# The end of the 3x3 stage: last banks divided by output half, one half's row sums added by TensorE

## The chip, the cores and the metric

One core of one Trainium2 chip runs the whole program. The metric is the device time of one execution in microseconds (us); lower is better. All arithmetic is fp32.

## The reference

Two ResNet bottleneck layers in sequence, on x of 64 x 1024 x 14 x 14, each with its own weights and with batch statistics (mean and variance over all 64 images and all pixels):

```
def _bn(x, gamma, beta):
    mean = jnp.mean(x, axis=(0, 2, 3), keepdims=True)
    var = jnp.var(x, axis=(0, 2, 3), keepdims=True)
    xn = (x - mean) * jax.lax.rsqrt(var + EPS)
    return gamma.reshape(1, -1, 1, 1) * xn + beta.reshape(1, -1, 1, 1)
out = jax.nn.relu(_bn(_conv(x, w1, b1, 1, 0), g1, be1))      # 1x1, 1024 -> 256
out = jax.nn.relu(_bn(_conv(out, w2, b2, 1, 1), g2, be2))    # 3x3,  256 -> 256
out = _bn(_conv(out, w3, b3, 1, 0), g3, be3)                 # 1x1,  256 -> 1024
out = jax.nn.softplus(residual_scale)[0] * out
return jax.nn.relu(x + out)
```

Because a norm needs the statistics of its whole input, no 1x1 product behind the 3x3 convolution can begin before the last pixel of the 3x3 convolution is summed and its statistics are merged. The change lies at exactly that border, which the program crosses twice, once in each layer.

## The kernel before

The 256 channels lie as 128 partitions x 2 halves (`MS` = 2; `o` is the output half, `s` the input half). The tile `y_all` holds all 256 channels of all pixels in SBUF, first the input of the 3x3 convolution and then, written back in place, its output. Images go in 8 groups of 8 (`NG` = 8, `GI` = 8).

`conv2` is the 3x3 stage. Along the rows it works with six combinations (`NF` = 6) of input rows, each multiplied with its own transformed filters; four output rows (`RT` = 4 tiles of rows, `out_rows[0]` to `out_rows[3]` and the bottom row `end`) are then sums and differences of the six products. The combinations come in pairs, in the order (1, 2), (3, 4), (5, 0), so combination 0 of group 7 is the last of the stage. Along the columns a product is done with even and odd output columns (`EVEN`, `ODD`, the index `q`): one product of sums (`m`), one of differences (`l`), and two more that are accumulated in PSUM onto a copy of `m`.

For one combination (`Products`) the pieces are these. `open` takes the PSUM tile `columns`: two banks of 512 fp32 values per partition, two such tiles in rotation. `start` makes `m` and `put` lets ScalarE copy it into both banks. `middle` makes `l`, and `bring` copies it with both signs to the SBUF tile `ls`. `columns` (the method) accumulates eight matmuls of 224 columns, two for each pair (`q`, `o`), into the banks; for the last combination it goes by output half (`across`): both `q` of `o` = 0, then both of `o` = 1. The trace counts two TensorE records for each fp32 matmul. Before the change the first index of the tile, the bank, is `q`, and the two output halves lie side by side in each bank.

`finish` is a generator that is sent each finished combination and forms the output rows. In the last group it pins the order of its VectorE work (`run`) and of ScalarE's (`act`), by hand. There `a` (tile `fa`) holds the sum of combinations 1 to 4, and `d` (tile `fb`) their weighted differences. Combination 5 completes `d` (line 1083), whose batch statistics are taken (`stat`, lines 1026 and 1085), and `merge` turns the sums of squares of the other rows into entries of the same table with GpSimd. Then combination 0, `cb`, completes `a`: line 1088 adds `cb.ls`, and lines 1089 to 1093 add the banks:

```
for o in range(MS):
    for q in EVEN, ODD:
        v = halves(a[:, o : o + 1])[:, q]
        run(nc.vector.tensor_add(v, v, cb.banks[:, q, o].rearrange("p (l c) -> p l c", c=WH)))
    stat(1, o, a)
```

Lines 1094 to 1097 let ScalarE copy the rows `d3`, `d[:, :, full]` and `a` to `y_all`. Meanwhile TensorE, which has nothing to compute, runs six matmuls of the identity into the tiles `m` (line 1240, `busy`).

Behind the stage `aggregate` (line 2079) merges the table with one `bn_aggr` for each output half, and `affine` makes scale and shift of it: a square root on ScalarE (`sd`, line 2095), then a row of small VectorE instructions (lines 2096 to 2127). The first rows of `y` are normed with them, on ScalarE (line 343, called through `norm`) and on VectorE (line 1595 in layer 0, 1353 in layer 1), and then the products of the third convolution start on TensorE (tiles `cy`, `cx`, `cp`).

Instructions that are neither pinned by `run` nor by `act` or `matmul` are put in an order by the framework, by their dependencies and by when they can be ready; it also inserts all waits between engines, from what each instruction reads and writes. `matmul` and `act` are helpers, so most TensorE work has line 168 and most ScalarE work line 343; go by the tile names.

Of the kernel before, what the change touches and what calls it, by code (L numbers as in the profile page):

```python
# [11 lines left out]
AF = mybir.ActivationFunctionType  # L12
# [7 lines left out]
MS = M // P  # L20
# [54 lines left out]
def bottlenecks(ctx: ExitStack, tc: tile.TileContext, x, w1s, w2s, w3s, pars, out):  # L75
# [633 lines left out]
    def conv2(b, par, aff, early, rest):  # L709
# [8 lines left out]
        def columns():  # L718

            return psum.pool.tile([P, 2, 512], FP, tag="columns", name="columns", bufs=2)  # L720
# [39 lines left out]
        class Inputs:  # L760
# [3 lines left out]
            def __init__(self, pair, run=lambda ins: None, copy=nc.scalar.activation):  # L764
                self.pair, self.run, self.copy = pair, run, copy
                self.tiles = tiles = full if pair[0] == 3 else RT
                self.lines = lines = tiles * GI
                n = len(pair) * MS * lines

                def part(tag, width):  # L770
                    v = place(tag, 2 * MS * RT * GI * width)
                    return v[:, : n * width].rearrange("p (k s l c) -> p k s l c", k=2, s=MS, c=width)

                self.r, self.v = part("r", W), part("v", W)
                self.sums, self.diffs = part("sums", WH), part("diffs", WH)
# [30 lines left out]
            def products(self, g, k):  # L806
                i = self.pair[k]

                first = g == 0 and i == order[0][0]
                u = {}  # L810
                for tag, a, e in ("ua", 0, 1), ("ub", 1, NK):
                    alone = made[tag] % BUFS[tag] == 0
                    made[tag] += 1
                    v = pool.tile(
                        [P, MS * MS * (e - a) * P], FP, tag=tag + "_first" * alone, name=tag, bufs=1 if alone else BUFS[tag] - 1
                    )
                    v = v.rearrange("p (s o k m) -> p s o k m", s=MS, o=MS, m=P)
                    for part in [slice(1, 2), slice(0, 1)] if g == 0 and i in order[0] else [slice(0, MS)]:
                        nc.sync.dma_start(
                            out=v[:, part].rearrange("p s o k m -> p (s o) (k m)"),  # L820
                            in_=us[b][i][:, part, :, a:e].rearrange("p s o k m -> p (s o) (k m)"),
                        )
                    u[a] = v
                return Products(i, self.lines, self.v[:, k], self.sums[:, k], self.diffs[:, k], u, first)

        def two_rows(g, s):
            v = y_all[:, s, g * GPX : g * GPX + 4 * full * LINE]
# [80 lines left out]
        class Products:  # L908


            def __init__(self, i, lines, r, sums, diffs, u, first):
                self.i, self.lines, self.n = i, lines, lines * WH
                self.r, self.sums, self.diffs, self.u, self.first = r, sums, diffs, u, first

            def bank(self, tag):
# [27 lines left out]

            def open(self):
                self.ls = None
                self.banks = columns()[:, :, : MS * self.n].rearrange("p q (o n) -> p q o n", o=MS)

            def fill(self):

# [66 lines left out]
        def finish():  # L1016


            for g in range(NG):
                out_rows = [y_grp[:, :, g, k::4, :] for k in range(4)]  # L1020
                last_group = g == NG - 1

                by_transfer = g < NG - 2

                def stat(k, o, v):
                    run(nc.vector.bn_stats(stats[:, o, 1 + k, :], v[:, o].rearrange("p r l -> p (r l)")))

                def run(ins):
                    tc.keep_in_program_order(ins)

                ca = yield
                fa = outputs(ca)
                if g == 1:
                    begin(y_grp[:, :, 0, 1 : 4 * full : 4, :])
                fb = outputs((yield))
                a, d = new("fa"), new("fb")
                nc.vector.tensor_add(a, fa, fb)
                nc.vector.tensor_sub(d, fa, fb)

                fa = outputs((yield))  # L1040
                fb = outputs((yield))
                c, e = new("fc", full), fa
                nc.vector.tensor_add(c, fa, fb)
                nc.vector.tensor_sub(e, fa, fb)
                a3, d3 = (v[:, :, :full] for v in (a, d))
                end = y_grp[:, :, g, H - 1]

                def middle_rows():

                    for o in range(MS):  # L1050
                        stt(out_rows[1][:, o, :full], e[:, o], 2.0, d3[:, o])
                        stt(out_rows[2][:, o], c[:, o], 4.0, a3[:, o])

                def outer_rows():

                    if by_transfer:

                        nc.vector.tensor_add(out_rows[0][:, :, :full], a3, c)
                        act(out_rows[0][:, :, full], a[:, :, full], AF.Copy)
                    else:  # L1060
                        nc.vector.tensor_add(a3, a3, c)
                    if by_transfer:

                        for o in range(MS):
                            stt(out_rows[3][:, o], e[:, o], 8.0, d3[:, o])
                        act(end, d[:, :, full], AF.Copy)
                    else:
                        stt(d3, e, 8.0, d3)

                if g > 1:  # L1070
                    middle_rows()
                    outer_rows()
                if last_group:
                    for o in range(MS):
                        lines = y_grp[:, o, g, 1 : 1 + 4 * full].rearrange("p (r k) l -> p r k l", k=4)[:, :, :2]
                        for k in range(2):
                            moment(lines, idle[:, : 2 * full * LINE].rearrange("p (r k l) -> p r k l", k=2, l=LINE), o, k, g)

                ca = yield
                if last_group:  # L1080

                    for v in ca.ls, ca.banks:
                        run(nc.vector.tensor_add(halves(d), halves(d), ca.by_columns(v)))
                    for o in range(MS):
                        stat(0, o, d)
                    merge()
                    cb = yield
                    run(nc.vector.tensor_add(halves(a), halves(a), cb.by_columns(cb.ls)))
                    for o in range(MS):
                        for q in EVEN, ODD:  # L1090
                            v = halves(a[:, o : o + 1])[:, q]
                            run(nc.vector.tensor_add(v, v, cb.banks[:, q, o].rearrange("p (l c) -> p l c", c=WH)))
                        stat(1, o, a)
                    act(out_rows[3], d3, AF.Copy)
                    act(end, d[:, :, full], AF.Copy)
                    for o in range(MS):
                        act(out_rows[0][:, o], a[:, o], AF.Copy)
                    continue
                fa = outputs(ca)
                if g < 2:  # L1100
                    outer_rows()

                if by_transfer:
                    for o in range(MS):
                        nc.gpsimd.dma_start(out=out_rows[3][:, o], in_=fa[:, o, :full], accum_op=ALU.add)  # L1105
                    nc.gpsimd.dma_start(out=end, in_=fa[:, :, full], accum_op=ALU.add)
                else:
                    nc.vector.tensor_add(out_rows[3], d3, fa[:, :, :full])
                    nc.gpsimd.tensor_add(end, d[:, :, full], fa[:, :, full])

                cb = yield
                if g < 2:
                    middle_rows()
                if by_transfer:

                    f = outputs(cb)
                    for o in range(MS):
                        nc.gpsimd.dma_start(out=out_rows[0][:, o], in_=f[:, o], accum_op=ALU.add)
                    continue
                nc.vector.tensor_add(halves(a), halves(a), cb.by_columns(cb.ls))  # L1120
                for q in (EVEN, ODD):
                    for o in range(MS):
                        to, more = (
                            v[:, o].rearrange("p r (i q c) -> p q r i c", i=GI, q=2)[:, q] for v in (out_rows[0], a)
                        )
                        nc.vector.tensor_add(to, cb.banks[:, q, o].rearrange("p (r i c) -> p r i c", r=RT, c=WH), more)
            yield
# [95 lines left out]
        for k in range(1, NG * NF):  # L1223
# [13 lines left out]
            item.columns(*qs, across=not more)  # L1237
            finished.send(item)
            queue = queue[1:] + list(itertools.islice(coming, k > 1))
        busy(psum, "m", 6)  # L1240

    def conv3(psum, t, o, w3, tag=None):
        ps = psum.tile(tag=tag)
# [1149 lines left out]
```

## Time and profile before

| what | us |
|---|---|
| median of 3 runs | 1884.51 |
| lowest and highest of them | 1884.0, 1885.09 |
| the profiled execution's own time | 1884.64 |
| its span, first to last instruction | 1882.9 |
| TensorE busy | 1867.9 (99% of the span) |
| VectorE busy | 1572.3 (84%) |
| ScalarE busy | 1111.8 (59%) |
| GpSimd busy | 744.1 (40%) |

Outside the span lie 1.7 us of the profiled execution. The stage ends at about 578.6 us of the span in layer 0 and at 1505.2 us in layer 1. A duration in a profile row belongs to one instruction or, with "xN", to N of them in a row; what stands in brackets behind it is idle time of that engine just before, and what ended it. In the chain of waits each piece is what the next one waited for.

### The profile page before, as it was taken

How to read it: one execution, taken by the hardware profiler on the slowest of the kernel's cores; microseconds unless marked ns; L12 is line 12 of the kernel's file. 1: busy time of each engine (PE TensorE's matmuls, PEld its weight loads, DVE VectorE, ACT ScalarE, POOL GpSimd, SP SyncE). 2: the span in 40 equal slices, each digit the busy share in tenths (PEclk: the TensorE clock that was granted, in tenths of full speed). 3: DMA queues.
4: the chain of work that ended last, by engine and by line, in shares of the span. 5: the costliest groups of instructions: out<-in, count | busy, mean ns of one | idle time of the engine just before them, and what ended most of it. 6: DMA issues, size and time to landing. Idle time of an engine off the chain costs nothing.

```text
span 1882.9 us, 28622 instructions
## 1 busy us (share of the span) xinstructions
PE 1867.9 (99%) x9728; PEld 1555.8 (83%) x9728; DVE 1572.3 (84%) x2494; ACT 1111.8 (59%) x2329; POOL 744.1 (40%) x763
## 2 busy tenths in 40 slices
PE   9999999999999999999999999999999999999999
PEld 5555557999998998899999999999999977555555
DVE  5787867999998776778878888899999987888887
ACT  2222214677777665555555555457777795766666
POOL 0111100121205655377677776301121051776665
PEclk9999999999999999999999999999999999999999
DMA  7777654797765556678788787559788466999997
GB/s 290 270 253 271 215 187 130 209 216 218 208 195 170 185 170 215 244 277 315 269 280 314 272 319 272 209 166 220 215 208 223 138 177 215 337 378 338 356 337 269
DMA packets 246754, 458.88 MB, mean 244 GB/s; under 512 B 41472, under 2 KB 213008, under 8 KB 233552
## 3 DMA queue, kind: packets, MB, share of 16 engines
q1 hardware_dynamic: 208432, 375.30, 59.1%
q0 software_dynamic: 31328, 29.18, 8.0%
q10 hardware_dynamic: 6848, 52.57, 6.9%
q8 instruction: 77, 1.26, 0.3%
q14 instruction: 69, 0.57, 0.1%
HBM read 289.44 MB, written 141.03 MB: 229 GB/s over the span
## 4 chain that ended last, share of the span: by engine, by line
PE 93%; DVE 4%; ACT 1%; issue 1%; POOL 0%; DMA 0%; ACTq 0%; SPq 0%; DVEq 0%; POOLq 0%
PE ay L168 20%; PE cy L168 16%; PE columns L168 13%; PE ap L168 13%; PE cp L168 8%; PE m L168 6%; PE l L168 6%; PE cx L168 5%; PE ax L168 4%; PE ps L168 1%; ACT y L343 0%; DMA x<-in_x 0%; DVE f L1004 0%; DVE v L796 0%; DVE y L751 0%
## 5 line engine op out<-in xcount | busy, mean ns | idle before, releaser
L168 PE MATMUL columns<-v,ub 128*128 128x224 f32 (+1 forms) x1536 | 303.4, 339 | 1.3 <-ACT columns L343 0.8
L343 ACT ACTIVATE x<-x,shift 128x392 f32<-128x392 f32 x444 | 255.2, 613 | 66.2 <-DVE x L537 31.4
L168 PEld LDWEIGHTS columns<-v,ub 128*128 128x128 f32 x1536 | 268.5, 188 | 8.3 <-ACT columns L343 1.5
L343 ACT ACTIVATE cu<-cy,scale 128x196 f32<-128x196 f32 (+1 forms) x360 | 175.6, 500 | 163.3 <-PE cy L168 156.2
L168 PE MATMUL ay<-at,ws 128*128 128x196 f32 (+1 forms) x760 | 191.6, 383 | 0.4 <-ACT au L343 0.2
L668 POOL TENSOR_TENSOR x<-x,cu 128x392 f32<-128x392 f32 x120 | 126.8, 1058 | 103.8 <-DVE x L537 68.2
L168 PEld LDWEIGHTS ay<-at,ws 128*128 128x128 f32 x760 | 134.8, 190 | 35.7 <-issue 1.0
L537 DVE SCALAR_TENSOR_TENSOR x<-cp,scale,x 128x196 f32<-128x196 f32 (+1 forms) x240 | 124.4, 518 | 42.0 <-PE cp L168 40.7
L343 ACT ACTIVATE au<-ay 128x196 f32<-128x196 f32 (+1 forms) x139 | 53.6, 386 | 169.6 <-PE ay L168 159.8
L168 PE MATMUL l<-diffs,ub 128*128 128x224 f32 (+1 forms) x768 | 149.7, 337 | 0.4 <-DVE diffs L804 0.3
L168 PE MATMUL m<-sums,ua 128*128 128x224 f32 (+1 forms) x752 | 146.0, 336 | 1.2 <-issue 0.6
L168 PEld LDWEIGHTS l<-diffs,ub 128*128 128x128 f32 x768 | 134.5, 189 | 1.8 <-DVE diffs L804 1.1
L1105 POOL DMA_DIRECT2D y<-f x24 | 32.1, 1635 | 258.4 <-DVE f L1004 258.4
L168 PEld LDWEIGHTS m<-sums,ua 128*128 128x128 f32 x752 | 131.4, 189 | 2.6 <-issue 0.9
L168 PE MATMUL cx<-y,w 128*128 128x196 f32 (+1 forms) x404 | 124.7, 395 | 0.0
L560 POOL TENSOR_TENSOR x<-x,cu 128x196 f32<-128x196 f32 (+1 forms) x120 | 104.9, 874 | 47.1 <-ACT cu L343 19.5
L168 PE MATMUL cy<-y,w 128*128 128x196 f32 (+1 forms) x372 | 115.5, 397 | 1.7 <-ACT y L343 0.9
L343 ACT ACTIVATE y<-y,shift,scale 128x320 f32<-128x320 f32 (+9 forms) x105 | 110.2, 1074 | 7.1 <-DVE shift L2127 6.4
L565 POOL TENSOR_TENSOR x<-x,cu 128x392 f32<-128x392 f32 x60 | 80.4, 1340 | 84.6 <-DVE x L537 81.9
L215 POOL DMA_DIRECT2D u<-y x48 | 26.0, 545 | 210.9 <-ACT y L343 210.1
L964 ACT ACTIVATE columns<-m 128x448 f32<-128x448 f32 (+1 forms) x144 | 70.8, 492 | 56.1 <-PE m L168 49.0
L1976 POOL TENSOR_SCALAR y<-y,scale 128x392 f32<-128x392 f32 x57 | 92.4, 1622 | 28.4 <-DVE scale L2334 28.4
(334 smaller groups left out, 4516.4 us busy)
## 6 DMA issues: line engine op xcount, KB each, us to landing
ub<-u SPq DMA_DIRECT2D x92, 768.0 KB, 5.4
x<-in_x SPq DMA_DIRECT2D x35, 1568.0 KB, 8.0
x<-mid SPq DMA_DIRECT2D x31, 1568.0 KB, 8.7
mid<-x ACTq DMA_DIRECT2D x30, 1568.0 KB, 9.3
out<-x SPq DMA_DIRECT2D x120, 392.0 KB, 7.1
x<-in_x SPq DMA_DIRECT2D x108, 392.0 KB, 7.9
ua<-u SPq DMA_DIRECT2D x92, 256.0 KB, 3.1
z<-kept SPq DMA_DIRECT2D x60, 392.0 KB, 3.0
```

The costliest lines, as they stand in the source:

```text
L168: tc.keep_in_program_order(nc.tensor.matmul(*args, **kw))
L215: nc.gpsimd.dma_start(out=us[b][i][:, s, o], in_=u)
L343: tc.keep_in_program_order(nc.scalar.activation(*args, **kw))
L537: run(nc.vector.scalar_tensor_tensor(v, bank, self.scale[:, o : o + 1], v, ALU.mult, ALU.add))
L560: run(nc.gpsimd.tensor_add(self.part(1, 1), self.part(1, 1), u3))
L565: run(nc.gpsimd.tensor_add(v, v, self.u12))
L668: nc.gpsimd.tensor_add(v, v, self.u12[:, i * self.n : (i + 1) * self.n])
L964: copy(v, m, AF.Copy)
L1105: nc.gpsimd.dma_start(out=out_rows[3][:, o], in_=fa[:, o, :full], accum_op=ALU.add)
L1976: run(nc.gpsimd.tensor_scalar(z, z, scale[:, o : o + 1], None, ALU.mult))
```

## The change

The last combination's two banks are divided by output half instead of by column parity: bank 0 holds both parities of `o` = 0, bank 1 those of `o` = 1. For `o` = 0, two matmuls of the identity with `a` (one for each parity) accumulate the row sums into bank 0, so that the finished row stands in PSUM; its `bn_stats` reads the bank, and ScalarE copies it from the bank to `y_all` in two pieces. For `o` = 1, VectorE adds bank 1 to `a` in one instruction instead of two, and takes the statistics and the copy from SBUF as before. Half 1 now comes ahead of half 0. `busy` runs four matmuls of the identity instead of six. The same code runs in both layers.

```
--- before.py
+++ after.py
@@ products
+                last = (g, i) == (NG - 1, order[-1][-1])
+                return Products(i, self.lines, self.v[:, k], self.sums[:, k], self.diffs[:, k], u, first, last)
...
@@ open
-                self.banks = columns()[:, :, : MS * self.n].rearrange("p q (o n) -> p q o n", o=MS)
+                v = columns()[:, :, : MS * self.n]
+                if self.last:
+                    self.banks = v.rearrange("p o (q n) -> p q o n", q=2)
+                else:
+                    self.banks = v.rearrange("p q (o n) -> p q o n", o=MS)
...
@@ finish, last group
                     run(nc.vector.tensor_add(halves(a), halves(a), cb.by_columns(cb.ls)))
-                    for o in range(MS):
-                        for q in EVEN, ODD:
-                            v = halves(a[:, o : o + 1])[:, q]
-                            run(nc.vector.tensor_add(v, v, cb.banks[:, q, o].rearrange("p (l c) -> p l c", c=WH)))
-                        stat(1, o, a)
+                    in_bank = [cb.banks[:, :, o].rearrange("p q (l c) -> p q l c", c=WH) for o in range(MS)]
+                    for q in EVEN, ODD:
+                        matmul(
+                            in_bank[0][:, q], ident, halves(a[:, :1])[:, q], start=False, stop=True, skip_group_check=True
+                        )
+                    v = halves(a[:, 1:])
+                    run(nc.vector.tensor_add(v, v, in_bank[1]))
+                    stat(1, 1, a)
+                    run(nc.vector.bn_stats(stats[:, 0, 2, :], cb.banks[:, :, 0].rearrange("p q n -> p (q n)")))
                     act(out_rows[3], d3, AF.Copy)
                     act(end, d[:, :, full], AF.Copy)
-                    for o in range(MS):
-                        act(out_rows[0][:, o], a[:, o], AF.Copy)
+                    act(out_rows[0][:, 1], a[:, 1], AF.Copy)
+                    for q in EVEN, ODD:
+                        act(
+                            out_rows[0][:, 0].rearrange("p r (i q c) -> p q r i c", i=GI, q=2)[:, q],
+                            cb.banks[:, q, 0].rearrange("p (r i c) -> p r i c", r=RT, c=WH), AF.Copy,
+                        )
                     continue
...
-        busy(psum, "m", 6)
+        busy(psum, "m", 4)
```

More of the change, by code (lines that the diff above doesn't have):

```diff
@@ L823, in products @@
                     u[a] = v
-                return Products(i, self.lines, self.v[:, k], self.sums[:, k], self.diffs[:, k], u, first)
+                last = (g, i) == (NG - 1, order[-1][-1])
+                return Products(i, self.lines, self.v[:, k], self.sums[:, k], self.diffs[:, k], u, first, last)
         def two_rows(g, s):
@@ L908, in conv2, with __init__ @@
         class Products:
-            def __init__(self, i, lines, r, sums, diffs, u, first):
-                self.i, self.lines, self.n = i, lines, lines * WH
+            def __init__(self, i, lines, r, sums, diffs, u, first, last):
+                self.i, self.lines, self.n, self.last = i, lines, lines * WH, last
                 self.r, self.sums, self.diffs, self.u, self.first = r, sums, diffs, u, first
```

## The prediction

> **What bounds the kernel now.** I read the page first: which engine carries the span, and whether TensorE's clock is granted throughout.
>
> ```profile
> PE 1867.9 (99%) x9728; PEld 1555.8 (83%) x9728; DVE 1572.3 (84%) x2494; ACT 1111.8 (59%) x2329; POOL 744.1 (40%) x763
> PEclk9999999999999999999999999999999999999999
> PE 93%; DVE 4%; ACT 1%; issue 1%; POOL 0%; DMA 0%; ACTq 0%; SPq 0%; DVEq 0%; POOLq 0%
> ```
>
> TensorE is busy for 99% and makes 93% of the chain that ended last; DVE has only 4% of it. So shorter DVE work pays only where TensorE's useful work waits for it. The change sits at such a place, and I read the chain of waits there, in layer 1:
>
> ```profile
> 1502.08 3.11 PE columns L168 x16
> 1505.19 0.02 issue
> 1505.21 0.70 DVE fa L1092 x2
> 1505.91 0.02 issue
> 1505.93 0.63 DVE stats L1026
> 1506.56 0.60 DVE fa L1092 x2
> ...
> 1507.18 0.63 DVE stats L1026
> 1507.81 0.28 DVE mv L2079 x2
> ...
> 1508.11 0.30 ACT sd L2095
> ...
> 1509.55 0.72 ACT y L343
> ...
> 1510.62 1.43 PE cy L168 x5
> ```
>
> From the last accumulation (1505.19) to the first product of the third convolution (1510.62) are 5.43 us in which no useful matmul runs. They are serial: four adds and two statistics on DVE, the merge, the root on ACT, scale and shift, one norm (the pieces left out). The page counts TensorE busy there because of the six idle-time matmuls of the identity. Whatever moves the root `sd` moves everything behind it. The same pieces stand in layer 0:
>
> ```profile
> 575.49 3.11 PE columns L168 x16
> 578.62 0.07 DVE fa L1092
> ...
> 581.21 0.28 DVE mv L2079 x2
> 581.51 0.30 ACT sd L2095
> ```
>
> From the end of the accumulation (578.60) to the root are 2.91 us, against 2.92 in layer 1 (1505.19 to 1508.11). So I work out layer 1 and count it twice. At most 2 x 2.9 us could be had here.
>
> **The change part by part.** The timeline of layer 1 has the single instructions:
>
> ```profile
> 1501.92 3.26 PE L168 MATMUL columns<-v,ub 128*128 128x224 f32 x16
> 1503.40 1.03 ACT L343 ACTIVATE y<-fb 128x672 f32<-128x672 f32 x2
> 1503.85 1.08 DVE L1088 TENSOR_TENSOR fa<-fa,ls 128x896 f32<-128x896 f32 x1
> 1504.83 0.38 PEld L168 LDWEIGHTS m<-ident 128*128 128x128 f32 x2
> 1505.02 4.69 PE L168 MATMUL m<-ident 128*128 128x448 f32 x12
> 1505.21 0.69 DVE L1092 TENSOR_TENSOR fa<-fa,columns 128x224 f32<-128x224 f32 x2 [0.28 <-PE columns L168]
> 1505.93 0.63 DVE L1026 BATCH_NORM_STATS2 stats<-fa 128x6 f32<-128x448 f32 x1
> 1506.48 0.67 DVE L1092 TENSOR_TENSOR fa<-fa,columns 128x224 f32<-128x224 f32 x2
> 1507.18 0.58 ACT L343 ACTIVATE y<-fa 128x448 f32<-128x448 f32 x1 [0.67 <-DVE fa L1092]
> 1507.18 0.63 DVE L1026 BATCH_NORM_STATS2 stats<-fa 128x6 f32<-128x448 f32 x1
> 1507.72 0.35 DVE L2079 BATCH_NORM_AGGREGATE mv<-stats 128x2 f32<-128x18 f32 x2
> 1508.11 0.30 ACT L2095 ACTIVATE sd<-mv,eps 128x2 f32<-128x2 f32 x1 [0.35 <-DVE mv L2079]
> ```
>
> And the mean times by form:
>
> ```profile
> L1092 DVE TENSOR_TENSOR fa<-fa,columns 128x224 f32<-128x224 f32 x4 | 1.4, 380 | 0.3 <-PE columns L168 0.3
> L1083 DVE TENSOR_TENSOR fb<-fb,columns 128x896 f32<-128x896 f32 x1 | 1.1, 1089 | 0.1
> L343 ACT ACTIVATE au<-ay 128x196 f32<-128x196 f32 x94 | 31.3, 333 | 36.8 <-PE ay L168 29.4 <-DVE y L441 7.4
> L343 ACT ACTIVATE au<-ay 128x392 f32<-128x392 f32 x45 | 22.3, 496 | 132.8 <-PE ay L168 130.4 <-DVE y L200 2.4
> L964 ACT ACTIVATE columns<-m 128x448 f32<-128x448 f32 x88 | 46.5, 528 | 46.9 <-PE m L168 40.8 <-DVE f L1004 4.6
> ```
>
> *TensorE, added:* two matmuls of the identity with 224 columns. The eight of the same width take 3.11 us, 0.389 each, so 0.78 for two, and the accumulation ends at 1505.97. They need `a` from L1088, which ends at 1504.93, 0.26 before TensorE gets there; that cover hides the wait and, just, one weight load (0.38 / 2 = 0.19). If it failed, the two loads of the first would be exposed, 0.38; I take 0 and keep 0.4 as the upper end.
>
> *TensorE, removed:* two of six idle-time matmuls, 4.69 / 6 = 0.78 each. Nobody reads them, so nothing on the path changes; TensorE's idle stretch before `cy` does (see the rivals).
>
> *DVE:* four adds and two statistics become one add and two statistics. The add of 448 values lies between 380 ns (224) and 1089 ns (896); on that line it takes 0.62. When may it start? Its own data, bank 1, are ready at 1505.19. But the trace shows how such a wait is counted. The first L1092 reads the `EVEN` bank, whose last writer is the sixth of eight matmuls, at about 1502.08 + 3.11 x 6/8 = 1504.41; DVE was free at 1504.93, and it still waited until 1505.21, the end of the eighth, which writes the other bank. So the wait is for the tile, not for the bank, and in the changed program the add is behind the two identity matmuls, which write the same tile ahead of it. Then: add 1505.99 to 1506.61; statistics of half 1 at 1506.63; statistics of half 0 at +0.55 (the step from 1505.93 to 1506.48), 1507.18; the merge at +0.54 (1507.18 to 1507.72), 1507.72. That is where it was: the 0.78 us taken from DVE come back as a wait for TensorE, to 0.01. A statistic from PSUM costs what it does from SBUF:
>
> ```profile
> L1613 DVE BATCH_NORM_STATS2 stats<-cy x2: 559/566/573, 586.4 to 590.1; 128x6 f32<-128x392 f32 x2
> L628 DVE BATCH_NORM_STATS2 stats<-kept 128x6 f32<-128x392 f32 x120 | 61.6, 553 | 0.0
> 585.87 0.50 ACT L343 ACTIVATE kept<-cy 128x392 f32<-128x392 f32 x1 [2.21 <-PE cy L168]
> 586.40 0.57 DVE L1613 BATCH_NORM_STATS2 stats<-cy 128x6 f32<-128x392 f32 x1 [1.60 <-ACT kept L343]
> ```
>
> *ACT:* the copy of half 1 starts at 1506.63 and ends by 1507.21 (0.58 as before). The two copies from the bank are new, and the last two rows show their wait: a statistic of `cy` began only when ACT's read of the same bank was over, so readers of one bank on two engines go one after the other. Here the statistic comes first: it ends at 1507.18 + 0.63 = 1507.81, and the copies start at 1507.82. Each has 224 values; on the line from 333 ns (196) to 496 ns (392) that is 0.36. Two in a row overlap by some 0.10 (the pair in the timeline at 1503.40, 0.75 and 0.38 long, took 1.03), so they end at 1507.82 + 0.62 = 1508.44. Queued behind them on ACT is the root, whose input is ready at 1508.09; it starts at about 1508.44 - 0.08 = 1508.36 instead of 1508.11. **+0.25 us a layer.** Upper end: copies like the 528 ns form, 0.95 for two, give 1508.69, +0.58, and with the exposed loads about +0.98. Lower end: if the root were put ahead of the copies, the merge decides and the layer gains or loses nothing.
>
> *What hangs on the root:* all of scale, shift, the norm and `cy`, and TensorE has no other useful work. Behind it the order is unchanged, so the shift stays to the end: 2 x 0.25 = +0.5. Against the profiled execution, 1884.64 (span 1882.9 and 1.7 around it), that is 1885.1; on the median, 0.13 lower, 1884.51 + 0.5 = **1885.0**. By its bounds the case gives 0 to +2.0, 1884.5 to 1886.5; the three runs shown spread over 1.1 us, so 1884.0 to 1887.0. About 0.2%, 3.8 us, is what a measurement of this kernel can tell from no change, and the forecast lies far inside that.
>
> **The rivals.** *The bank counts, not the tile.* Then bank 1 is free at 1505.19 and the division does what it can: add 1505.21, statistics 1505.85 and 1506.40, merge 1506.94; the copies start at 1507.04 and the root at 1507.58, -0.53 a layer, -1.1 in all: 1883.4. For it speaks that with the halves in separate banks nothing physical stands between the add and the identity matmuls; against it, the 0.28 us wait of L1092, in both layers. The Trainium skill, PSUM — Partial Sum Buffer, section "PSUM bank collisions raise a hardware error", has the rule that goes with it: guard by bank, since accesses to different banks run clean. The chip would allow it by that; the row shows the program ordering more.
>
> *The clock is lost.* The idle-time matmuls now end at 1505.97 + 4 x 0.78 = 1509.1, and `cy` starts at 1510.9: 1.8 us without a matmul where there were 0.9 with the clock at 1.00:
>
> ```profile
> 1509.70:1510.60 0.90, 0.01 (x1) 0.01 (x1) 0.86 (x3) 0.90 (x2) 0.00 (x0) 1.00 0.00 0
> ```
>
> If a gap of that length halves the clock, and it takes as much work to get it back as the six matmuls (4.69 us), that work takes twice as long: +4.7 a layer, +9.4, 1894. It decides once the gap is over whatever the gate allows; no stretch of this trace shows that limit, only that 0.9 us is under it. The Trainium skill, TensorE: Matmul & The Clock Gate, section "What's actually happening", puts it at one idle window of about 3.4 us, by which the gap would be short enough; no run here shows that yet.
>
> *The order elsewhere moves.* Unpinned work behind the border is placed by when it can be ready. If instructions of layer 0's next stage change places, TensorE may gain or lose some waits; all its idle time together is 1882.9 - 1867.9 = 15 us, so I give this case up to 5 us either way, 1880 to 1890.
>
> **How the numbers follow.** The forecast has 0.67, the rival with the bank 0.15, the lost clock 0.06, a moved order 0.12. The forecast's range and the bank's 1883.4 with half the runs' spread below it make 1882.8 to 1887.0, which leaves out the lost clock and most of the moved order. Within 0.2%: 0.67 + 0.15 + 0.03 of the moved order = 0.85. Slower: 0.06 + 0.04 = 0.10. Faster: 0.05, all from a moved order.
>
> **What would show it.** In the profile after, the add of 448 values should start some 0.8 us behind the last `columns` matmul of the accumulation, with TensorE as its releaser, and take 0.6; both statistics should follow with no gap; the two ACT copies from the bank should start when the second statistic ends, and the root right behind them, not behind the merge. An add that starts with the end of the accumulation, while TensorE still works on the identity, shows the bank rival. A granted clock under 1.00 after either border shows the lost clock. If the root sits as I say and the time still differs by over 2 us, the cause lies outside this border and the working is wrong in what it leaves out.

## The result, and the profile after

The changed kernel takes 1888.3 us in the median of 22 executions (1885.07 to 1890.19); the kernel before, measured beside it, takes 1884.95 (22 executions, 1884.0 to 1886.76). The ratio is 1.0014, with an interval of [1.0008, 1.002]: 3.35 us slower, where the prediction had 1885.0 and a range up to 1887.0. The profiled execution took 1888.97 us, its span is 1887.2 (before 1884.64 and 1882.9).

The border first. The timeline of layer 1, changed kernel:

```profile
1503.74 3.26 PE L168 MATMUL columns<-v,ub 128*128 128x224 f32 x16
1506.83 1.00 PE L168 MATMUL columns<-fa,ident 128*128 128x224 f32 x4
1507.67 3.18 PE L168 MATMUL m<-ident 128*128 128x448 f32 x8
1507.87 0.62 DVE L1100 TENSOR_TENSOR fa<-fa,columns 128x448 f32<-128x448 f32 x1 [1.13 <-PE columns L168]
1508.52 0.63 DVE L1031 BATCH_NORM_STATS2 stats<-fa 128x6 f32<-128x448 f32 x1
1509.07 0.62 DVE L1102 BATCH_NORM_STATS2 stats<-columns 128x6 f32<-128x448 f32 x1
1509.79 0.33 DVE L2092 BATCH_NORM_AGGREGATE mv<-stats 128x2 f32<-128x18 f32 x2
1509.80 0.62 ACT L343 ACTIVATE y<-columns 128x224 f32<-128x224 f32 x2 [0.70 <-DVE stats L1102]
1510.30 0.29 ACT L2108 ACTIVATE sd<-mv,eps 128x2 f32<-128x2 f32 x1
```

The add does wait for TensorE (1.13 us), behind the identity matmuls; the copies from the bank start when the second statistic ends; the root follows the copies. In the chain of waits of layer 1 the same place reads:

```profile
1503.90 3.95 PE columns L168 x20
1507.85 0.02 issue
1507.87 0.63 DVE fa L1100
...
1509.15 0.54 DVE stats L1102
...
1509.80 0.62 ACT y L343 x2
1510.42 0.18 ACT sd L2108
...
1512.81 2.83 PE cy L168 x6
```

The sixteen products of the accumulation took 3.11 us before, so here they end at 1503.90 + 3.11 = 1507.01, and the root starts 3.29 us later, where it was 2.92 before: +0.37 a layer.

The last row holds what the prediction did not expect. Six matmuls of `cy` take 2.83 us. Before they took 1.75, and TensorE had been idle for 0.91 us ahead of them (timeline of the kernel before):

```profile
1510.62 1.75 PE L168 MATMUL cy<-y,w 128*128 128x196 f32 x6 [0.91 <-ACT y L343]
```

The page still shows nine tenths of clock in every slice, since a slice is 47 us long. Cut into pieces of 3.41 us around both borders, the trace shows it (windows view; per row the window, its length, then busy time and count for PE, PEld, DVE, ACT and POOL, then the granted clock):

```profile
core 0: us, PE busy (x) PEld busy (x) DVE busy (x) ACT busy (x) POOL busy (x), PEclk, DMA share, GB/s
577.98:581.39 3.41, 3.41 (x14) 2.11 (x13) 2.21 (x7) 0.73 (x2) 1.75 (x13) 1.00 0.07 22
581.39:584.80 3.41, 1.57 (x6) 0.54 (x4) 2.93 (x16) 1.34 (x4) 0.00 (x0) 1.00 0.00 0
584.80:588.22 3.42, 3.42 (x7) 2.16 (x8) 0.79 (x3) 1.11 (x3) 0.00 (x0) 0.50 0.00 0
588.22:591.63 3.41, 3.41 (x12) 2.02 (x11) 3.38 (x5) 2.37 (x5) 3.24 (x3) 1.00 0.24 90
...
1509.81:1513.23 3.42, 1.46 (x5) 0.49 (x3) 2.94 (x16) 2.28 (x6) 0.00 (x0) 1.00 0.44 184
1513.23:1516.64 3.41, 3.41 (x7) 2.17 (x7) 3.22 (x9) 3.41 (x7) 2.15 (x4) 0.50 0.29 70
1516.64:1520.05 3.41, 3.41 (x12) 1.96 (x11) 1.45 (x5) 3.41 (x5) 2.43 (x5) 1.00 0.81 201
```

The clock is lost at both borders. It is halved for one step of 3.41 us, and the drop begins after useful matmuls have come back (`cy` starts at 584.08 and 1512.81, the drops at 584.80 and 1513.23). The two drops start 928.43 us apart, which is 272 steps of 3.4133. So the boundaries lie on one grid that runs through the whole execution, and each drop follows a window in which TensorE was idle for 3.41 - 1.57 = 1.84 us and 3.42 - 1.46 = 1.96 us, a little over half of it.

Comparing the starts of the same instructions in both traces gives the account of the span:

| place | after minus before, us | step |
|---|---|---|
| ahead of layer 0's border | -0.15 | |
| first `cy` of layer 0 | +0.21 | +0.37 border |
| behind the drop in layer 0 | +1.73 | +1.52 clock |
| ahead of layer 1's border | +1.82 | +0.09 |
| first `cy` of layer 1 | +2.19 | +0.37 border |
| behind the drop in layer 1 | +3.67 | +1.48 clock |
| from 1613 on | +4.36 | +0.69 (see the last section) |

That is the difference of the spans, 4.3 us. Outside the two borders TensorE, VectorE, ScalarE and GpSimd have their instructions in the same order as before.

### The profile page after: what moved, and what is told of

It reads as the page before. It is cut to its first block, busy times and chain, and to the rows that moved or that the text cites. A ratio compares the mean times of both kernels' runs of the same rounds, so it can differ in the third digit from the quotient of the medians.

```text
span 1887.2 us, 28621 instructions
## 1 busy us (share of the span) xinstructions
PE 1869.2 (99%) x9728; PEld 1558.0 (83%) x9728; DVE 1572.4 (83%) x2488; ACT 1111.3 (59%) x2331; POOL 741.9 (39%) x763
## 3 DMA queue, kind: packets, MB, share of 16 engines
q8 instruction: 77, 1.26, 0.3%
## 4 chain that ended last, share of the span: by engine, by line
PE 93%; DVE 4%; ACT 1%; issue 1%; POOL 1%; DMA 1%; SPq 0%; DVEq 0%; ACTq 0%; POOLq 0%
PE ay L168 20%; PE cy L168 16%; PE columns L168 14%; PE ap L168 13%; PE cp L168 8%; PE m L168 6%; PE l L168 6%; PE cx L168 5%; PE ax L168 4%; PE ps L168 1%; DMA x<-in_x 0%; DVE f L1009 0%; ACT y L343 0%; DVE v L796 0%; DVE y L751 0%
```

## The experiments

The medians in the table are of 11 executions (22 for the change itself); those of the kernel before, measured beside them, are of 15 to 33. The runs e1 to e4 shared one chip, e5 to e8 a second, e9 to e11 a third, and e12 had a fourth, so a difference is taken to the kernel before of the same row. "Clock" counts the executions with a mean granted clock of 1.000 / 0.999 / 0.998. One lost window costs 3.41 x 0.5 / 1885 = 0.0009 of the mean. A 0.999 alone says little, since the kernel before shows it in one execution of ten: a trace can also end in a piece at half clock, behind the last matmul, and that counts in the mean (1.92 us of the changed kernel's).

| kernel | median | before | difference | ratio, interval | clock |
|---|---|---|---|---|---|
| the change | 1888.3 | 1884.95 | +3.35 | 1.0014 [1.0008, 1.002] | 8/8/6 |
| e1: six idle-time matmuls | 1886.83 | 1884.83 | +2.00 | 1.0008 [0.9999, 1.0017] | 10/1/0 |
| e10: e1 again | 1885.97 | 1885.24 | +0.73 | 1.0005 [0.9996, 1.0014] | 11/0/0 |
| e2: before with four | 1886.69 | 1884.83 | +1.86 | 1.0009 [1.0, 1.0017] | 0/8/3 |
| e3: the change with five | 1886.40 | 1884.83 | +1.57 | 1.0006 [0.9997, 1.0014] | 11/0/0 |
| e12: four in two pairs | 1885.94 | 1884.44 | +1.50 | 1.0008 [0.9999, 1.0017] | 9/2/0 |
| e4: two tiles, first form | 1884.63 | 1884.83 | -0.20 | 0.9995 [0.9987, 1.0004] | 10/1/0 |
| e5: two tiles | 1885.40 | 1884.59 | +0.81 | 1.0004 [0.9995, 1.0013] | 9/2/0 |
| e6: two tiles, root first | 1884.54 | 1884.59 | -0.05 | 1.0 [0.9992, 1.0009] | 10/1/0 |
| e11: e6 again | 1884.97 | 1885.24 | -0.27 | 0.9999 [0.999, 1.0008] | 8/3/0 |
| e9: e6 with late x | 1884.73 | 1885.24 | -0.51 | 0.9997 [0.9989, 1.0006] | 10/1/0 |
| e7: e1 with late x | 1885.46 | 1884.59 | +0.87 | 1.0005 [0.9996, 1.0014] | 10/1/0 |
| e8: before with late x | 1885.20 | 1884.59 | +0.61 | 1.0003 [0.9995, 1.0012] | 9/2/0 |

**Is it the clock, and the idle-time matmuls that were taken out?** The change with all six of them (e1, and e10 once more later):

```
-        busy(psum, "m", 4)
+        busy(psum, "m", 6)
```

> The changed kernel with six idle-time matmuls of the identity instead of four. Theory of the clock: TensorE's stretch without work ahead of the first product of the third convolution shrinks from 1.8 to 2.0 us to about 0.3 us, the granted clock stays at 1.000 in every run, and the time falls from 1888.3 to before plus twice 0.37 us, about 1885.7, with a spread as small as that of the kernel before (under 3 us). Theory of the border's own chain or of moved work elsewhere: those stay as they are, and the time stays at about 1888.

> The changed kernel with six idle-time matmuls and the early x once more, now on the chip on which the late x is compared. If the stall at about 740 us belongs to the kernel, 1886.5 or more, as in its first call; if it belongs to the chip or the hour, about 1885.5, as the late x gave.

The clock is back: one execution of 22 is under 1.000. In e1's trace the border costs +0.37 in each layer and nothing follows it; the row that answers to the 2.0 us of the changed kernel (waits view), and the clock (cores view):

```profile
PE cy L168 <- ACT y L343: 0.4, 1, 0.4
core 0: 1883.1 us, clock 1.000
```

So the change without the loss of the clock is +0.37 twice. In e10 the median says the same, +0.73. In e1 it was +2.00, and the 1.26 us on top stay open: the trace of e1 is of its fastest execution, 1884.88, and shows nothing of them. The stall of ACT that the expectation of e10 speaks of (more on it below) does not settle it, since e10's own trace has that stall, 1.11 us, and its median is low all the same. Its 1885.97 lies between the two values expected and decides for neither.

**Does the loss need the rest of the change?** The kernel before, with four idle-time matmuls in place of six and nothing else:

```
-        busy(psum, "m", 6)
+        busy(psum, "m", 4)
```

> The kernel before with four idle-time matmuls instead of six and nothing else. Theory of the clock: the stretch without work grows from 0.9 to about 2.5 us, the clock falls to half for 3.4 us behind some or both borders in most runs, and the time rises by 1.5 to 3.5 us in those runs, to 1886.5 to 1888.5, although the root starts where it did. Theory of the border's own chain: nobody reads these matmuls, so the time stays at 1884.9.

No. None of its 11 executions kept a mean clock of 1.000, where 98 of 108 of the kernel before did, and the root is where it was. The time alone is weaker evidence: +1.86 us, with an interval that reaches 1.0. The trace says most about the rule, since its two borders went different ways (windows on the grid of that trace, as above):

```profile
578.45:581.86 3.41, 2.76 (x8) 1.09 (x6) 3.19 (x14) 1.45 (x3) 1.22 (x11) 1.00 0.00 0
581.86:585.27 3.41, 1.73 (x7) 1.12 (x8) 2.38 (x11) 0.71 (x1) 0.00 (x0) 1.00 0.02 5
585.27:588.69 3.42, 3.42 (x12) 2.03 (x11) 2.65 (x4) 2.55 (x6) 1.93 (x2) 1.00 0.00 0
1506.87:1510.29 3.42, 1.00 (x4) 0.30 (x3) 3.10 (x16) 1.93 (x5) 0.27 (x6) 1.00 0.62 261
1510.29:1513.70 3.41, 3.41 (x8) 2.33 (x9) 3.20 (x9) 3.41 (x7) 1.46 (x2) 0.50 0.14 33
```

In layer 1 a gap of 2.42 us lies in one window, and the next window has half the clock. In layer 0 a gap of 2.27 us, nearly as long, lies across a boundary, so that the two windows hold 0.65 and 1.68 us of idle time (0.06 of it in short pauses), and the clock stays at 1.00. So the length of the gap does not decide alone: its place on the grid does too.

**Where is the limit?** The change with five:

```
-        busy(psum, "m", 4)
+        busy(psum, "m", 5)
```

> The changed kernel with five idle-time matmuls. The stretch without work becomes 1.0 to 1.2 us. If the gate lets the clock go once less than about half of one 3.4 us window is work, no run loses it, and the time is that of six, about 1885.7. If any gap beyond the 0.9 us of before is enough, some runs show a clock under 1.000 and 1887 or more.

All 11 executions are at 1.000. (The median is still +1.57. The traced execution is 2.18 us above that of the kernel before, and of this the borders are 0.73 and the stall described below 1.41.) The gaps are 1.0 and 1.2 us; the window with the longer one, and the kernel before's own beside it:

```profile
1510.14:1513.55 3.41, 2.21 (x8) 0.92 (x7) 2.93 (x15) 2.27 (x7) 0.00 (x0) 1.00 0.33 137
```

```profile
1507.35:1510.77 3.42, 2.51 (x8) 1.06 (x7) 3.09 (x17) 1.93 (x5) 0.27 (x6) 1.00 0.62 259
```

A closer bound stands at the end of e1's trace, where the last matmuls run out. One window there has 3.42 - 1.65 = 1.77 us of idle time, and the next one, without any matmul, still has the full clock:

```profile
1877.23:1880.65 3.42, 1.65 (x9) 1.21 (x8) 1.47 (x3) 1.75 (x4) 0.00 (x0) 1.00 0.92 345
1880.65:1883.10 2.45, 0.00 (x0) 0.00 (x0) 0.00 (x0) 0.00 (x0) 0.00 (x0) 1.00 0.13 45
```

Together: idle times of 0.91, 1.20, 1.68 and 1.77 us in a window kept the clock; 1.84 (a gap of 1.80 and short pauses), 1.96 and 2.42 lost it. So in these traces the limit lies between 1.77 and 1.84 us, a little over half a window (1.71); the profile models the ends of matmuls, so the last hundredths are not certain. As an estimate, take 1.8: a gap of 1.84 us has over 1.8 in one window for (3.41 - 1.84) + 2 x 0.04 = 1.65 of 3.41 possible places, 48%; one of 1.96 for 52%. If the two borders were independent, 75% of the executions would lose the clock at least once, 16 or 17 of 22; 14 of the changed kernel's 22 were below 1.000. The eight at 1.000 have a median of 1885.84, 0.89 over before, about the two borders; the six at 0.998 have 1889.22.

**One long gap, or idle time summed over a window?** The four idle-time matmuls in two pairs, the second behind the merge:

```
-        busy(psum, "m", 4)
+        busy(psum, "m", 2)
...
+            mv2 = aggregate(stats2, 0)
+            for _ in range(2):
+                matmul(ps2.tile(448, "m"), ident, mv2[:, 0, :1].to_broadcast([P, 448]), start=True, stop=True)
```

> The changed kernel with its four idle-time matmuls in two pairs: the second pair reads the merged statistics and so starts behind the merge. TensorE's idle time between the accumulation and the first product stays at about 2.0 us but is cut into two gaps of about 1 us each. Theory A (the granted clock goes by TensorE's idle share of a window of 3.413 us, and both gaps can lie in one): the clock is still lost in a good part of the executions, granted clock 0.998 or 0.999 in about half of them, those executions 1.5 us longer for each border that lost it, median 1886.5 to 1888.5. Theory B (what decides is the longest single gap, and gaps up to 1.2 us kept the clock): 1.00 in all executions and 1885.5 to 1886.

This did not tell them apart. The clock was kept, and the traced execution, 1.39 us above that of the kernel before, has 0.73 of it at the borders and 0.69 at one VectorE add (last section). The second pair took 1.75 us, so the gaps came out smaller than planned:

```profile
1508.57 1.75 PE L168 MATMUL m<-mv,ident 128*128 128x448 f32 x4 [0.83 <-DVE mv L2092]
1511.21 1.76 PE L168 MATMUL cy<-y,w 128*128 128x196 f32 x6 [0.89 <-ACT y L343]
```

The gaps are 0.83 + 0.89 = 1.72 us here, of which 1.63 lie in one window of the grid, and 1.56 in layer 0, on two sides of a boundary. The clock was kept, as theory B has it; but theory A with a limit of 1.8 gives the same. Whether two short gaps add up stays open.

**Is it the tile that the add waits for?** First form: the last combination's two halves in two tiles of one bank each. It leaves out part of the last combination's sum in one half, so its time is to be read with care. Then (e5) with combination 5's product `m` written to its bank in two parts (`part`), after which both halves accumulate in full:

```
-                    self.banks = v.rearrange("p o (q n) -> p q o n", q=2)
+                    self.halves = [columns()[:, 0, : 2 * self.n].rearrange("p (q n) -> p q n", q=2), None]
...
+                    self.halves[1] = psum.tile(2 * self.n, "m").rearrange("p (q n) -> p q n", q=2)
...
+                m = self.bank("m")
+                for s in reversed(range(MS)):
+                    self.part(m, SUM, self.sums, s)
...
-        busy(psum, "m", 4)
+        busy(psum, "l", 5)
```

> The changed kernel with the two halves of the last combination in two separate PSUM tiles of one bank each instead of one tile of two, and five idle-time matmuls (so that the stretch without work is about 0.2 us). Theory that the add waits for the tile: the add now starts 0.02 us behind the end of the accumulation instead of 0.86, while TensorE works on the identity, the root starts at about 2.46 us behind that end instead of 3.29 (before: 2.92), and the time is 1884.95 minus twice 0.46, about 1884.0. Theory that TensorE's writes themselves hold the add, whatever the tile: add and root stay where they are, and the time is that of six idle-time matmuls, about 1885.7.

> The last combination's two halves lie in two tiles of one bank each instead of one tile of two banks, and combination 5's bank is written in two parts so that both halves accumulate; five idle-time matmuls, in another bank. Theory (the wait is counted by tile, and the rest of the change works as meant): the add of 448 values starts at the end of the accumulation, not 0.86 us behind it, and the root comes about 2.35 us behind that end (before 2.92, the change 3.29): -0.57 a layer, a span 1.1 below the kernel before, unless the x transfers hold ACT at about 740 us of the span, which cost 1.3 us in the run of the first two-tile kernel: 1883.7 without that stall, 1884.8 with it, clock 1.00. Rival (the wait has another cause and the first two-tile kernel was early only because its sums were incomplete): the add starts 0.8 us late again and the time is about 1886.

The timeline of e5, layer 1:

```profile
1504.67 1.02 PE L168 MATMUL columns<-fa,ident 128*128 128x224 f32 x4
1504.87 0.62 DVE L1115 TENSOR_TENSOR fa<-fa,m 128x448 f32<-128x448 f32 x1 [0.26 <-PE m L168]
...
1506.72 0.62 ACT L343 ACTIVATE y<-columns 128x224 f32<-128x224 f32 x2 [0.61 <-DVE stats L1117]
...
1507.22 0.29 ACT L2123 ACTIVATE sd<-mv,eps 128x2 f32<-128x2 f32 x1
```

The add starts while TensorE is at the identity matmuls, and the root comes 2.35 us behind the add's start. TensorE's position against before goes from -0.09 to -0.66 in layer 0 and from -0.33 to -0.89 in layer 1, 0.57 and 0.56 earlier. The wait was for the tile, shown in both forms: half 1 had a bank of its own in the changed kernel too, and only the tile is new. The median did not follow: +0.81.

**What is left of the delay, and can it be had?** e6 puts the two ACT copies behind the root and lets the merge take half 1 first, with four idle-time matmuls:

```
-        for o in range(n):
+        for o in reversed(range(n)):
...
+        if late_copies:
+            run(root)
...
+        while late_copies:
+            late_copies.pop(0)()
```

> As the two-tile kernel, with two orders changed: the two ACT copies from the bank are put behind the root, and the merge takes half 1, whose statistics are ready first, ahead of half 0; four idle-time matmuls. Theory (copies ahead of the root and the merge's order are what is left of the delay): the root comes 2.1 to 2.2 us behind the end of the accumulation, -0.75 a layer against the kernel before, 1883.3; TensorE's gap in front of the first product is about 0.9 us and the clock stays at 1.00. Rival (the norm needs the copies anyway and gets later by what the root gains): the first product is no earlier than in the two-tile kernel. The stall at about 740 us may add 1.3 to either.

```profile
1506.37 0.62 DVE L1116 TENSOR_TENSOR fa<-fa,m 128x448 f32<-128x448 f32 x1 [0.26 <-PE m L168]
...
1508.10 0.37 DVE L2112 BATCH_NORM_AGGREGATE mv<-stats 128x2 f32<-128x18 f32 x2
...
1508.51 0.30 ACT L2128 ACTIVATE sd<-mv,eps 128x2 f32<-128x2 f32 x1 [0.91 <-DVE mv L2112]
1508.71 0.60 ACT L343 ACTIVATE y<-columns 128x224 f32<-128x224 f32 x2
```

The root is 2.14 us behind the add's start, with the clock at 1.00. In layer 0 the first product gains 0.79 us against before. In layer 1 the root gains about as much, but the first product waits for its weights `w` (timeline up to 1512):

```profile
1511.44 0.74 PE L168 MATMUL cy<-y,w 128*128 128x196 f32 x3 [1.23 <-DMA w<-in_w]
```

This transfer is issued at 1506.50, 0.15 us behind the end of the accumulation, and takes 4.8 us to land, as in before's trace, where the norm was ready later. So the first product gains 0.34 us, and the products from `cx` on 0.53, where e5 had gained 0.46 and 0.55. The rival of the expectation holds in layer 1, through a cause that it did not name: the first product comes no earlier than with two tiles alone, however early the root is. Yet of the 0.79 + 0.53 us that e6's trace gains at the borders the median shows nothing, 1884.54 against 1884.59; the next runs ask where they go.

**Who gives it back?** In e6's trace 1.65 us come back near 740, where ACT waits for the write of a result, `z<-kept`, before it may fill that slot again. The write stands in a queue with the x transfers of the next images, issued just before it. Late x: their issue moved behind it, in three kernels.

```
-                if unit in (44, 48):
+                if unit in (56, 57):
```

> The changed kernel with six idle-time matmuls, as in the first run of this study, and with the x transfers of the next images issued at units 56 and 57 of the layer instead of 44 and 48. Theory (the 1.2 us by which that first kernel's median lies above its border's cost is the stall of ACT on a transfer that queues behind x, in part of its executions): 1885.6, and hardly an execution above 1886.5. Rival (the extra has another cause): 1886.8 as before. A second risk: the later x is waited for in layer 1, which would show as a wait of its first readers and add to the time.

> The kernel before with the x transfers at units 56 and 57: the control of the run above. Theory (the stall at about 740 us is rare in the kernel before): 1884.8, no change. Rival (the later x costs by itself): slower by more than 1 us, and the same amount is then in the run above.

> The kernel with two tiles, the copies behind the root and the reversed merge, with the x transfers at units 56 and 57. Theory (the border gives 2 x 0.79, and the stall at about 740 us takes most of it back): no stall there, the drift against the kernel before stays at -0.8 behind layer 0 and -1.6 behind layer 1: 1883.0 to 1883.3 in the median, about 1.2 below the same kernel with the early x. Rival (the later stage absorbs an earlier start whatever the x transfers do): 1884.5, as with the early x.

> The kernel with two tiles, the copies behind the root and the reversed merge once more, with the early x, beside its twin with the late x: 1884.5 with the stall in most executions, against 1883.2 for the twin. Rival (the x transfers are not what makes the stall): both the same.

The twins e11 (early x) and e9 (late x), the same unit on ACT, and the transfers issued from 725 to 745 (KB each, median us to landing):

```profile
742.31 0.33 ACT L343 ACTIVATE kept<-ay 128x196 f32<-128x196 f32 x1 [3.06 <-DMA z<-kept]
```

```profile
x<-in_x SPq DMA_DIRECT2D x2, 1568.0 KB, 9.0
z<-kept SPq DMA_DIRECT2D x6, 392.0 KB, 4.4
```

```profile
738.52 0.33 ACT L343 ACTIVATE kept<-ay 128x196 f32<-128x196 f32 x1 [0.62 <-PE ay L168]
```

```profile
z<-kept SPq DMA_DIRECT2D x7, 392.0 KB, 2.8
```

The traces agree with the theory but are too few to show it: the stall is there in five of eleven with the early x (e3, e4, e6, e10 and e11, 1.1 to 1.65 us each) and in none of the three with the late x, which would happen by chance about one time in four. It is not a part of the change: it comes with a later and with an earlier border, and e5, with the early x, does not have it. In the medians nothing shows: e9 is 0.24 us below its twin e11, and e8 0.61 above before, both inside the intervals; e7's +0.87 is no lower than e10's +0.73 with the early x. e9 missed its 1883.0 to 1883.3.

The trace of e9 shows other places where a gain ends. Its position against before is -0.79 behind the border of layer 0, as expected, but -1.01 and not -1.6 behind that of layer 1: 0.35 is lost between them, and the second border gains only 0.57, with the wait for `w` again. At the end it is +0.08. Of this way back, 0.37 us go where DVE waits for the transfer that brings `y` into the tile `home`, and 0.70 at the VectorE add of the last section. In e5's layer 1 the wait for `home` costs 0.74, and before's trace does not have it there (waits view, 1525 to 1560):

```profile
DVE zt L1338 <- DMA home<-y: 2.0, 1, 2.0
```

An earlier start is not needed for it: e8, whose border is unchanged, loses 0.55 at the same place.

No version beats the kernel before by what can be measured; e9, 0.9997 [0.9989, 1.0006], is nearest.

## Why the prediction was wrong

*The working of the border was right in kind.* The add waited for the tile, with TensorE as its releaser; the statistics followed without a gap; the copies stood ahead of the root. A statistic from PSUM took 0.62 us, as from SBUF. The size was off by 0.12 a layer: +0.37 and not +0.25. The two identity matmuls took 3.95 - 3.11 = 0.84 and not 0.78, and the copies started 0.11 us behind the end of the statistic (1509.69 to 1509.80) where 0.01 was taken; the root started 0.12 ahead of the copies' end (1510.30 and 1510.42), where 0.08 was taken. The merge came later than the prediction had it, because its first half is the one whose statistic ends last, but the copies covered that.

*The step that failed is the term "TensorE, removed": the prediction put the two idle-time matmuls at nothing on the path, and gave the rival "the clock is lost" a chance of 0.06.* Without them the clock was lost in most executions, and in the traced one this cost 1.52 and 1.48 us. The prediction had the gap right, 1.8 us (1.84 and 1.96 measured), and the place to look. It then let the limit rest on the only case at hand, 0.9 us without a loss, and on the rule that goes with it. The Trainium skill, TensorE: Matmul & The Clock Gate, section "What's actually happening", gives a window of 3413 ns that runs freely and returns the clock to half after an idle window. The trace agrees with the grid and its length, 3.413 us; it does not agree with an idle window in the sense of one without work: 54% idle (1.84 of 3.41 us) was enough. What the rows of before left open was the limit itself, anywhere above 0.9 us, and a gap of twice that length deserved far more than 0.06.

*The price was off the other way.* 4.7 us a layer came from work taking twice as long until the clock is back. In all three drops at a border that were traced it came back after one window. TensorE had work in all of that window, but at half clock 3.41 us do only the work of 3.41 x 0.5 = 1.71, so a loss costs at most 1.71 us, and 1.52 and 1.48 were measured.

*Two other rivals.* "The bank counts, not the tile" fell in the changed kernel. What it would have brought is what e5 shows once the tiles are apart: 0.57 a layer, where 0.53 was worked out. "The order elsewhere moves" did not happen.

*The range* left out the lost clock: +0.74 for the borders and about 3.0 for two lost windows make up the profiled execution's excess but 0.6, for which the VectorE add of the last section, +0.69, accounts. The executions that kept the clock have a median of 1885.84, inside the range.

## What to carry over

Matmuls without a reader may be part of the timing: before they are taken out, set TensorE's longest idle stretch against a window of 3.413 us, and keep it under half of one; here 1.77 us kept the clock and 1.84 lost it. Two banks in one tile are one thing to wait for, so dividing work between banks pays only when the tile is divided as well. A gain in the middle of a stage is only had if what comes next can start earlier too: in e6 the root gained 0.8 us and the first product of layer 1 only 0.34, because its weights were still on their way. Follow the shift to the end of the span, not to the end of the border.

## What was not expected of the hardware

The clock is taken away late: on a boundary of the 3.413 us grid, which in the changed kernel's trace lies 0.72 and 0.42 us behind the return of the matmuls (0.10 us in e2's), and for one step of the grid only. So the penalty falls mostly on useful work, and the same program loses the clock in some executions and keeps it in others.

The step of +0.69 in the account is a single DVE instruction. One add `ct` in layer 1 takes 0.57 us in before's trace and in eight others, and 1.45 us in five, those of the change, e8, e9, e11 and e12. In e8 the border is unchanged, so the step does not come from there. The traces show what goes with it: in all 14 a GpSimd add `x<-x,cu` starts 0.02 to 0.03 us behind `ct`. In the nine, `ct` is the short one and the GpSimd add takes 1.41 to 1.43 us; in the five, the GpSimd add takes 1.00 to 1.01 and `ct` the 1.45. Timelines of before and of e8:

```profile
1606.90 0.57 DVE L503 TENSOR_TENSOR ct<-ct,y 128x392 f32<-128x392 f32 x1
1606.93 1.42 POOL L668 TENSOR_TENSOR x<-x,cu 128x392 f32<-128x392 f32 x1
```

```profile
1607.39 1.45 DVE L503 TENSOR_TENSOR ct<-ct,y 128x392 f32<-128x392 f32 x1
1607.41 1.00 POOL L668 TENSOR_TENSOR x<-x,cu 128x392 f32<-128x392 f32 x1
```

So in each trace one of the two adds is held up by the other: the one held up ends about 0.4 us (`ct`) or 0.9 us (the GpSimd add) behind it. What decides which is held up, between starts that lie hundredths of a microsecond apart, stays open.
